# Gathering turned attention rows through a DRAM scratch: one write and four reads in place of sixteen transfers inside SBUF

## The chip, the core and the metric

The kernel runs on one core of a Trainium2 chip. The metric is device time in microseconds (us), the median of the runs. The compute engines are TensorE (PE in the profile, its weight loads PEld), VectorE (DVE), ScalarE (ACT) and GpSimd (POOL). Each works through its own instructions in order. SyncE (SP, its queue SPq) issues nearly all DMA transfers of this kernel, also in order: an issue that waits holds up every issue behind it. The transfers themselves run on sixteen DMA engines.

## The reference

One transformer block with adaptive layer norm, on 8 sequences of 1024 tokens and 512 channels, 16 heads of 32 channels, causal attention, all in float32:

```python
mod = jax.nn.silu(condition) @ Wada + bada
sh_a, sc_a, gt_a, sh_m, sc_m, gt_m = jnp.split(mod, 6, axis=1)
xn = _layernorm(x, g1, be1)
xm = xn * (1.0 + sc_a[:, None, :]) + sh_a[:, None, :]
x = x + gt_a[:, None, :] * _attention(xm, Wqkv, Wproj, bproj)
xn = _layernorm(x, g2, be2)
xm = xn * (1.0 + sc_m[:, None, :]) + sh_m[:, None, :]
h = jax.nn.gelu(xm @ W1 + b1, approximate=False)
x = x + gt_m[:, None, :] * (h @ W2 + b2)
```

## The kernel before

The 8192 rows are cut into 16 blocks of 512 tokens, two to a sequence. For each block the kernel normalizes the rows, brings them into a layout with channels on the partitions, modulates them (the tile xm_a), projects k, q and v, attends, projects out (Wproj), and does the same for the MLP half (xm_m, then up and down). Products with the large weights are done by Strassen's scheme: seven products of half-size blocks in place of eight, with sums of weight blocks (S1 to S4, kept in DRAM as kept_qkv, kept_up and kept_down) and differences of activation blocks (T1 to T4, the tile t_a).

The program is put in order by a planner inside the kernel. It keeps a clock for each engine (now), the planned time at which a value is there (written) and at which a buffer is free (left). Work that is to be interleaved is written as generators ("threads"): each yields what it needs next, and the planner advances the one whose wait is shortest. A number such as GATHERING = 16000 (ns) in written is an assumption on when a transfer will have landed. It moves instructions in the program's order; on the chip the engines wait on semaphores, whatever was assumed.

Weights come through a ring of nine buffers (RING, the tile w, 256 KB a piece). fetch() issues the next piece as soon as a buffer is released in the program's order, so on the chip a fetch (lines 338, 340 and 342) waits in SyncE's queue for the TensorE product that last read the buffer. In the same queue stand the x loads (line 389), the loads of the residual xr (line 1262), the gate rows (line 512) and the stores of finished rows to the output (line 1098). A store waits for the last addition to xr (line 161 on GpSimd: xr<-xr,p_d for the first pair of row tiles stored, xr<-xr,y_d for the second).

The attention rows of blocks 0 and 1 are turned by TensorE. Those of blocks 2 to 15 are "turned" without it, in fourteen turns, each in the generator turn():

1. The rows come in by four loads, so that partitions 32t to 32t+31 hold four rows each (line 389: the destination is 32 partitions by 4 by 512). They are normalized in place (the tile hat_a).
2. turn_tile (line 664): VectorE transposes blocks of 32 by 32, four instructions a block, from hat_a to xm_a, which serves as a scratch here.
3. The gathering (line 673): sixteen transfers, one for each pair of a group of 32 source partitions and a group of 32 target partitions, bring the pieces back to hat_a, 64 KB each.
4. modulated() then reads hat_a and writes xm_a, one chunk of channels at a time (line 726 on VectorE or line 732 on ScalarE), and forms the differences T1 to T4 (lines 740, 742, 158 and 161).

At about the time of a turn TensorE finishes the down products of an earlier block, then goes to the v products of the next and, between their last two, to the output projection (w with qT). Line 193 is the combine by VectorE that takes a product out of its PSUM bank.

The generators that matter are these:

Of the kernel before, what the change touches and what calls it, by code (L numbers as in the profile page):

```python
# [9 lines left out]
F32 = mybir.dt.float32  # L10
# [12 lines left out]
def kernel(  # L23
# [33 lines left out]
    nc = tc.nc  # L57
    B, T, D = x.shape
    HD = W1.shape[1]
    P = 128  # L60
# [3 lines left out]
    NTT = TB // P  # L64
# [18 lines left out]
    kept = ctx.enter_context(tc.tile_pool(name="kept", bufs=1, space=bass.MemoryType.DRAM))  # L83
# [10 lines left out]
    now = {"PE": 0.0, "DVE": 0.0, "ACT": 0.0, "POOL": 0.0}  # L94
    written, left = {}, {}
# [16 lines left out]
    def note(engine, ns, reads=(), writes=(), port=False):  # L112
        start = max(now[engine], due(reads, writes))
        if port:
            start = max([start] + [b for a, b in pool_spans if a <= start < b])
        end = start + ns
        now[engine] = end
        if engine == "POOL":
            pool_spans.append((start, end))
            del pool_spans[:-16]  # L120
        for k in reads:
            left[k] = max(left.get(k, 0.0), end + SYNC)
        for k in writes:
            written[k] = end + SYNC
        return end
# [102 lines left out]
    def mlp_steps(n):  # L228
        return [("u", n, i) for i in range(NQ)] + [("d", n, part) for part in range(4)]
# [9 lines left out]
    for w in range(1, NB):  # L239
        n = w - 1  # L240
        m = mlp_steps(n)
# [125 lines left out]
    rows = tmp.tile([P, TB], F32, tag="y", name="rows")[:n_rows, :P]  # L367
# [8 lines left out]
    Q = P // NTT  # L376
# [141 lines left out]
    def add_job(job, reads, first=False):  # L518

        at = sum(1 for other in jobs if other[2]) if first else len(jobs)  # L520
        jobs.insert(at, (job, reads, first))
# [134 lines left out]
    def turn(key, rows, xm):  # L656

        small_blocks = xm.rearrange("p c n -> p (c n)")
        by_tile = small_blocks.rearrange("p (m h t i) -> p h m t i", m=NTT, h=NC, t=NTT)
        written["blocks", key] = NEVER  # L660

        def turn_tile(t):
            into = by_tile[:, :, :, t, :]
            nc.vector.transpose(into, rows[:, t, :].rearrange("p (h m i) -> p h m i", m=NTT, i=Q))
            done = [("blocks", key)] if t == NTT - 1 else []
            note("DVE", 620, [("hat", key, t)], done)

        for t in range(NTT):
            add_job(lambda t=t: turn_tile(t), [("hat", key, t)], key[0] == "m")
        yield [("blocks", key)], []  # L670
        for m in range(NTT):
            for a in range(NTT):
                nc.sync.dma_start(rows[ts(m, Q), a, :], small_blocks[ts(a, Q), ts(m, D)])  # L673
        written["turned", key] = now["PE"] + GATHERING
        yield [("turned", key)], []

    GATHERING = 16000

    def modulated(key, gain, shift, b, guards):
        for t in ("B11", "B21", "B22", "T1", "T2", "T3", "T4"):  # L680
# [22 lines left out]
        if turned:  # L703
            yield from turn(key, got, xm)
# [1204 lines left out]
```

## Time and profile before

| | |
|---|---|
| median of 3 runs | 3577.96 us (3577.63 to 3582.41) |
| profiled execution, from its first to its last instruction | 3570.9 us |
| TensorE busy | 3495.3 us, 98% |
| VectorE / ScalarE / GpSimd busy | 61% / 33% / 58% |
| granted TensorE clock, mean | 0.997 |
| DMA queue of SyncE and ScalarE | 439.36 MB, 41.7% of sixteen engines' span |
| HBM read / written | 394.12 MB / 28.38 MB |

The profile is of one execution. Rows of the waits name who waited for whom, the total in us, how often, and the longest. Rows in order of time give start and duration in us, engine, line, operation, tiles (out<-in), shapes, count, and in brackets the idle time before and what ended it. Rows by stretch give the stretch and its length, then for each engine its busy time and instructions (PE, PEld, DVE, ACT, POOL), the granted clock, the share of time in which the DMA engines were busy, and GB/s. In the source view of a line three durations stand for the shortest, the median and the longest, in ns. Rows of the chain of waits give start, duration and what the end was waiting on. Issuing instructions on SyncE show the time of the issue, not of the transfer.

### The profile page before, as it was taken

To read this page: it belongs to the slowest core of one execution; us is meant where nothing else is said; L and a number is where in the kernel's file an instruction comes from. 1 tells how busy PE (TensorE), PEld (TensorE's weight loads), DVE (VectorE), ACT (ScalarE), POOL (GpSimd) and SP (SyncE) were. 2 spreads that over 40 slices of the span, in tenths; PEclk is the share of its full clock that TensorE was granted. 3 is DMA by queue.
4 is the path that set the end of the run, shared out by engine and by line. 5 is a ranking of instruction groups with operands and counts; after the bars stand their busy time and mean duration, and the time that the engine had idled before them with its cause. 6 is when DMAs were issued, how large, how long until landed. Compare 5 with 4: busy or idle time off the path is not lost.

```text
span 3570.9 us, 120927 instructions
## 1 busy us (share of the span) xinstructions
PE 3495.3 (98%) x54621; PEld 1749.3 (49%) x54621; DVE 2179.7 (61%) x2393; ACT 1187.1 (33%) x1232; POOL 2080.9 (58%) x2246
## 2 busy tenths in 40 slices
PE   8999899999999999999999999999999999999999
PEld 4444445445554445545454455544545445455445
DVE  5876575564755657465574656746666566565663
ACT  2334333242333513235142342423423134231421
POOL 2667746665466664667545775366762667526660
PEclk9999999999999999999999999999999999999999
DMA  6753433434434344433444334443344433434334
GB/s 200 235 174 93 128 93 110 135 105 138 115 109 131 108 141 113 135 107 105 142 118 146 99 101 141 120 140 102 102 131 124 140 105 104 126 111 140 91 113 137
DMA packets 318934, 447.12 MB, mean 125 GB/s; under 512 B 29516, under 2 KB 179852, under 8 KB 318164
## 3 DMA queue, kind: packets, MB, share of 16 engines
q1 hardware_dynamic: 318304, 439.36, 41.7%
q8 instruction: 430, 7.05, 0.8%
q14 instruction: 84, 0.69, 0.1%
q10 hardware_dynamic: 116, 0.03, 0.0%
HBM read 394.12 MB, written 28.38 MB: 118 GB/s over the span
## 4 chain that ended last, share of the span: by engine, by line
PE 88%; POOL 4%; DMA 3%; DVE 2%; SPq 2%; issue 1%; ACT 1%; ACTq 0%; DVEq 0%; POOLq 0%
PE bank L202 60%; PE sc L1511 8%; PE po L1644 7%; PE st L1604 7%; PE st L1592 2%; POOL pT L1734 2%; PE bank L1665 2%; DMA w<-in_L_cond_Wproj_dram 1%; PE bank L722 1%; SPq L673 1%; POOL hT L161 1%; DVE mx L1528 1%; DMA out_dram<-xr 0%; PE bank L1566 0%; DMA w<-in_L_cond_Wada_dram 0%
## 5 line engine op out<-in xcount | busy, mean ns | idle before, releaser
L1734 POOL TENSOR_TENSOR pT<-pT,pT 128x256 f32<-128x256 f32 (+3 forms) x1254 | 1215.4, 1005 | 335.5 <-PE po L1644 182.2
L1616 ACT ACTIVATE pT<-st 128x2048 f32<-128x2048 f32 x288 | 541.0, 1878 | 1171.6 <-PE st L1604 1074.2
L202 PE MATMUL bank<-w,hT 128*32 128x256 f32 x14336 | 813.0, 380 | 1.1 <-ACT rec L1674 0.9
L1528 DVE TENSOR_REDUCE mx<-sc 128x4 f32<-128x2048 f32 (+3 forms) x384 | 665.8, 1754 | 223.3 <-PE sc L1511 217.1
L202 PEld LDWEIGHTS bank<-w,hT 128*32 128x32 f32 x14336 | 453.0, 110 | 365.7 <-issue 81.0
L202 PE MATMUL bank<-xm_m,w 128*32 128x256 f32 x8192 | 498.2, 380 | 0.0
L202 PE MATMUL bank<-t_m,w 128*32 128x256 f32 x6144 | 383.4, 380 | 0.1
L1621 POOL TENSOR_SCALAR_AFFINE_SELECT pT<-pT 128x512 f32<-128x512 f32 x256 | 168.1, 675 | 344.6 <-ACT pT L1616 344.6
L202 PEld LDWEIGHTS bank<-xm_m,w 128*32 128x32 f32 x8192 | 257.2, 110 | 219.9 <-issue 54.6
L1511 PE MATMUL sc<-kT,qT 32*128 32x512 f32 (+3 forms) x3072 | 329.1, 520 | 2.7 <-DVE mx L1528 1.7
L1525 DVE TENSOR_TENSOR sc<-sc,mask 128x1024 f32<-128x1024 f32 (+1 forms) x160 | 162.7, 1017 | 265.5 <-PE sc L1511 177.5
L1644 PE MATMUL po<-pT,v 128*32 128x512 f32 (+3 forms) x3048 | 303.0, 492 | 2.1 <-POOL pT L1621 2.1
L1604 PE MATMUL st<-qT,kT 32*128 32x512 f32 (+3 forms) x3072 | 301.5, 488 | 0.0
L202 PEld LDWEIGHTS bank<-t_m,w 128*32 128x32 f32 x6144 | 190.2, 110 | 180.8 <-issue 58.1
L202 PE MATMUL bank<-w,qT 128*32 128x512 f32 x2048 | 240.7, 599 | 10.6 <-DMA w<-in_L_cond_Wproj_dram 10.5
L202 PE MATMUL bank<-xm_a,w 128*32 128x256 f32 x3968 | 246.0, 383 | 2.1 <-ACT p_k L188 2.0
L1683 DVE RECIPROCAL rec<-rec 128x128 f32<-128x128 f32 x256 | 224.5, 918 | 33.0 <-ACT rec L1674 33.0
L1511 PEld LDWEIGHTS sc<-kT,qT 32*128 32x128 f32 x3072 | 129.3, 183 | 173.1 <-ACT pT L1616 65.7
L202 PE MATMUL bank<-t_a,w 128*32 128x256 f32 x2944 | 189.6, 382 | 0.4 <-ACT xm_m L732 0.4
L193 DVE TENSOR_TENSOR hT<-bank,u_u 128x512 f32<-128x512 f32 x192 | 129.1, 684 | 98.2 <-PE bank L202 96.9
L1058 ACT ACTIVATE hT<-hT,cols 128x512 f32<-128x512 f32 x256 | 164.4, 711 | 54.6 <-DVE hT L193 54.0
L202 PEld LDWEIGHTS bank<-xm_a,w 128*32 128x32 f32 x3968 | 123.6, 110 | 110.8 <-issue 33.4
(216 smaller groups left out, 3405.6 us busy)
## 6 DMA issues: line engine op xcount, KB each, us to landing
w<-in_L_cond_W_dram SPq DMA_DIRECT2D x384, 256.0 KB
w<-kept_up_S SPq DMA_DIRECT2D x256, 256.0 KB
w<-kept_down_S SPq DMA_DIRECT2D x256, 256.0 KB
w<-kept_qkv_S SPq DMA_DIRECT2D x180, 256.0 KB
w<-in_L_cond_Wqkv_dram SPq DMA_DIRECT2D x147, 256.0 KB
hat_a<-in_x_dram SPq DMA_DIRECT2D x64, 256.0 KB
w<-in_L_cond_Wproj_dram SPq DMA_DIRECT2D x64, 256.0 KB
xr<-in_x_dram SPq DMA_DIRECT2D x64, 256.0 KB
```

The source lines that it names most:

```text
L193: nc.vector.tensor_tensor(out, src, other, op)
L202: nc.tensor.matmul(ps[r, :], columns, rhs, start=start, stop=stop, skip_group_check=True)
L1058: nc.scalar.activation(hT[:, i, :], hT[:, i, :], AF.Gelu, bias=cols[:, O_B1 + f : O_B1 + f + 1])
L1511: nc.tensor.matmul(sc[:, j, c0 : c0 + w], qTs[n][r, gg, ts(qt, P)], keys_of(n, kh)[r, gg, :w], start=True, stop=True, skip_group_check=True,)
L1525: nc.vector.tensor_tensor(place, place, shape_of.to_broadcast(place.shape), ALU.add)
L1528: nc.vector.tensor_reduce(maxima[n, gg][:, kh, qt, :], sc[:, :, c0 : c0 + w], axis=AX.X, op=ALU.max)
L1604: nc.tensor.matmul(st[:, j, c0 : c0 + w], kT[r, gg, ts(k % NTT, P)], qT[r, gg, TB - w :], start=False, stop=True, skip_group_check=True,)
L1616: nc.scalar.activation(pT[:, :, :used], st[:, :, :used], AF.Exp, scale=scale)
L1621: nc.gpsimd.affine_select(diagonal, diagonal, pattern=[[0, HPG], [1, P]], compare_op=ALU.is_ge, fill=0.0, base=0, channel_multiplier=-1,)
L1644: nc.tensor.matmul(po[r, TB - w :], v[:, k % NTT, g * P + j * hd : g * P + (j + 1) * hd], pT[:, j, c0 : c0 + w], start=(k == 0), stop=last ...
L1683: nc.vector.reciprocal(some, some)
L1734: nc.gpsimd.tensor_tensor(into, into, pT[:, j, c0 : c0 + w], ALU.add)
```

## The change

The sixteen transfers go. In their place the whole scratch (128 partitions by 8 KB) is written to a DRAM tile in one transfer, and four transfers read it back, each to 32 partitions, four rows of 2 KB to a partition, the form of the x loads. Two DRAM tiles alternate. Between write and reads the generator yields, so that the planner can put other work there; it assumes 8 us for the write and 8 us for the reads, where it assumed 16 us for the gathering. The reads wait on the chip for the write to have landed.

```diff
         yield [("blocks", key)], []
+        held = kept.tile([P, NTT * D], F32, tag=f"held_{turns[0] % 2}", name=f"held_{key}")
+        turns[0] += 1
+        nc.sync.dma_start(held, small_blocks)
+        written["held", key] = now["PE"] + HOLDING
+        yield [("held", key)], []
         for m in range(NTT):
-            for a in range(NTT):
-                nc.sync.dma_start(rows[ts(m, Q), a, :], small_blocks[ts(a, Q), ts(m, D)])
-        written["turned", key] = now["PE"] + GATHERING
+            some = held[:, ts(m, D)].rearrange("(a i) d -> i a d", i=Q)
+            nc.sync.dma_start(rows[ts(m, Q), :, :], some)
+        written["turned", key] = now["PE"] + HOLDING
         yield [("turned", key)], []
 
-    GATHERING = 16000
+    HOLDING = 8000
+    turns = [0]
```

In the order of instructions that results, the four reads stand four to nine transfers behind the write. For most blocks these are weight fetches and one or two pairs of output stores: in the turns of blocks 4 to 10 the reads come behind the first pair and ahead of the second, in those of blocks 11, 12 and 14 behind both, and in those of blocks 13 and 15 behind the last pair (the other being ahead of the write). On the compute engines the order is nearly the same as before; some dozen instructions at the modulation, the v combines and the output projection change places or engines, among them one chunk of the modulation in most blocks.

## The prediction

> **What bounds the kernel now.** I read the page first, then who waited for whom on TensorE, then the source view of the gather line, then SyncE in order of time around one turn.
>
> ```profile
> span 3570.9 us, 120927 instructions
> PE 3495.3 (98%) x54621; PEld 1749.3 (49%) x54621; DVE 2179.7 (61%) x2393; ACT 1187.1 (33%) x1232; POOL 2080.9 (58%) x2246
> ```
> ```profile
> PE bank L202 <- DMA w<-kept_qkv_S: 11.7, 7, 2.2
> PE bank L202 <- DMA w<-in_L_cond_Wproj_dram: 10.5, 12, 1.9
> ...
> PE bank L202 <- DMA w<-in_L_cond_Wqkv_dram: 3.7, 1, 3.7
> ```
>
> TensorE sets the end: it is idle for 75.6 us in all (3570.9 − 3495.3), so no edit that leaves its own work alone can win more. Three rows of its waits are for weight pieces, 11.7 + 10.5 + 3.7 = 25.9 us in 20 waits. Where they come from is seen on SyncE (start, duration, engine, line, operation, tiles, count) around the turn of block 7:
>
> ```profile
> L673 SPq DMA_DIRECT2D hat_a<-xm_a x224: 507/588/2077, 130.6 to 3051.9; - x112
> ```
> ```profile
> 1283.09 0.34 SPq L340 DMA_DIRECT2D w<-kept_qkv_S  x1
> 1283.57 11.66 SPq L673 DMA_DIRECT2D hat_a<-xm_a  x16
> 1295.32 1.02 SPq L340 DMA_DIRECT2D w<-kept_qkv_S  x2
> 1296.43 0.85 SPq L1098 DMA_DIRECT2D out_dram<-xr  x2
> ...
> 1297.89 0.89 SPq L338 DMA_DIRECT2D w<-in_L_cond_Wqkv_dram  x1
> 1298.87 1.05 SPq L342 DMA_DIRECT2D w<-in_L_cond_Wproj_dram  x2
> 1300.01 0.87 SPq L1098 DMA_DIRECT2D out_dram<-xr  x2
> 1300.97 1.79 SPq L342 DMA_DIRECT2D w<-in_L_cond_Wproj_dram  x2
> ```
> ```profile
> 1284.00:1295.00 11.00, 11.00 (x212) 6.62 (x208) 1.38 (x2) 0.00 (x0) 6.22 (x6) 1.00 0.47 116
> 1297.00:1302.00 5.00, 5.00 (x100) 2.84 (x93) 1.96 (x3) 3.37 (x5) 0.00 (x0) 1.00 0.99 314
> ```
>
> The sixteen issues hold SyncE for 11.66 us, while the DMA engines are busy 0.47 of the time at 116 GB/s (last two columns). Issue binds there, not data. The weight fetches, whose ring slots TensorE frees meanwhile, stand behind, go out in a burst that fills the engines (0.99), and TensorE runs dry some 20 us after the turn began:
>
> ```profile
> 1290.03 1.29 POOL L161 TENSOR_TENSOR xr<-xr,p_d 128x512 f32<-128x512 f32 x1
> 1295.64 1.28 POOL L161 TENSOR_TENSOR xr<-xr,y_d 128x512 f32<-128x512 f32 x1
> 1299.12 2.92 ACT L732 ACTIVATE xm_a<-hat_a,shifta,gaina 128x512 f32<-128x512 f32 x4
> 1303.41 1.28 DVE L193 TENSOR_TENSOR v<-bank,u_v 128x512 f32<-128x512 f32 x2
> 1305.22 1.92 PE L202 MATMUL bank<-w,qT 128*32 128x512 f32 x16 [1.37 <-DMA w<-in_L_cond_Wproj_dram]
> 1307.68 1.92 PE L202 MATMUL bank<-w,qT 128*32 128x512 f32 x16 [0.54 <-DMA w<-in_L_cond_Wproj_dram]
> 1309.42 1.91 PE L202 MATMUL bank<-w,t_a 128*32 128x256 f32 x32
> ```
>
> The same rows asked for by stretch, first 612 to 1960 us (the turns of blocks 4 to 10), then 2150 to 2835 us (blocks 11 to 14), then block 13's turn alone (2596 to 2630 us):
>
> ```profile
> PE bank L202 <- DMA w<-in_L_cond_Wproj_dram: 7.5, 9, 1.4
> PE bank L202 <- DMA w<-kept_qkv_S: 5.5, 3, 2.2
> ```
> ```profile
> PE bank L202 <- DMA w<-kept_qkv_S: 6.1, 4, 2.0
> PE bank L202 <- DMA w<-in_L_cond_Wproj_dram: 3.0, 3, 1.9
> ```
> ```profile
> PE bank L202 <- DMA w<-in_L_cond_Wproj_dram: 1.9, 1, 1.9
> ```
>
> So 13.0 us fall to blocks 4 to 10, 9.1 − 1.9 = 7.2 us to blocks 11, 12 and 14, 1.9 us to block 13, and the one wait for Wqkv, 3.7 us, to block 15; the turns of blocks 2 and 3 have none.
>
> **What the change removes.** 224 issues of 588 ns (median), 14 × 16. In their place stand 14 × 5. Their cost has near rows: the one transfer of 1 MB is the move of a whole kT, 0.51 us, and the four gathers have the form of the x loads (32 partitions by four rows of 2 KB), 1.84 us for four.
>
> ```profile
> 436.69 0.51 SPq L972 DMA_DIRECT2D kT<-kT_early  x1
> ```
> ```profile
> 1382.38 1.84 SPq L389 DMA_DIRECT2D hat_a<-in_x_dram  x4
> ```
> ```profile
> 438.00:440.00 2.00, 0.99 (x12) 0.31 (x8) 0.00 (x0) 1.00 (x1) 2.00 (x3) 1.00 1.00 376
> 1384.00:1388.00 4.00, 4.00 (x48) 1.25 (x40) 0.38 (x1) 2.84 (x3) 0.64 (x1) 1.00 1.02 237
> ```
>
> So 11.66 us of SyncE become 0.51 + 1.84 = 2.35 us. If nothing came in their place, all 25.9 us of waits for weights would go.
>
> **What it adds: data.** A turn moves 1.05 MB out and 1.05 MB back, where it moved 1.05 MB once. At the kT move's rate (376 GB/s, engines full) the write takes 2.8 us; at the x loads' rate (237 GB/s, also full, 32 partitions a transfer) the reads take 4.4 us, and I take 4.8 because fetches of the faster kind were mixed into that window. What a transfer costs beside its data: the last gather of block 15 was issued at 3051.88 and its reader began at 3054.52, 2.6 us with 0.3 us of data, so about 2.3 us.
>
> ```profile
> 3051.88 0.94 SPq L673 DMA_DIRECT2D hat_a<-xm_a  x1
> ```
> ```profile
> 3054.52 2.22 ACT L732 ACTIVATE xm_a<-hat_a,shifta,gaina 128x512 f32<-128x512 f32 x3 [6.76 <-DMA hat_a<-xm_a]
> ```
>
> **What it adds: two waits on SyncE.** First, the reads wait for the write. It lands 2.3 + 2.8 = 5.1 us after its issue on an empty queue. No row shows a 1 MB write to DRAM; the lower bound is this 5.1 us, the upper one the longest store in the chain (6.56 us for 256 KB in a full queue, its data replaced by the write's): 6.56 − 0.7 + 2.8 = 8.7 us. In the changed program four to nine transfers stand between write and reads, and among them, in most turns, a store to the output that waits for GpSimd. So SyncE comes to the reads 8 us or more behind the write, and I cost this wait at 0, its upper end at 0.7 us. Its cover is the work of those fetches and stores.
>
> ```profile
> 2820.36 6.56 DMA out_dram<-xr
> ```
>
> Second, those stores. They were reached after the sixteen issues, when their data were ready. Now SyncE reaches the first pair at once and must wait for xr<-xr,p_d, which in block 7's turn ends at 1291.32, 7.8 us after the write. The fetches behind this pair stay late, though by 7.8 and not 11.7 us. Worked for block 7: write 1283.57, stores 1291.3 to 1292.2, three fetches to 1293.6, reads 1293.6 to 1295.4. Ahead of them 5 × 0.26 MB need 3.5 us of engine time, a backlog of 1.3 us. The reads land at 1293.6 + 1.3 + 2.3 + 4.8 = 1302.0. The Wproj pieces, issued at 1293.1, 1295.4 and, behind the second stores (1296.9), about 1298.3 and 1298.8, land before 1305.9, against use at 1303.8 to 1306.4 without the gaps. That is enough, with under half a microsecond to spare for the last two.
>
> **What is late next.** The reads land at 1302.0, but ScalarE wanted them at 1299.12: it now stands 2.9 us. VectorE stands too, and queued behind its part of the modulation are the three differences and the combine v (1303.41), which frees what TensorE's next product (1309.42) writes to. From landing to the end of the first combine I count 2.2 (three ACTIVATEs) + 3 × 0.72 = 4.4 us, so 1306.4. TensorE without its two gaps comes to that product at 1309.42 − 1.91 = 1307.5: covered, by 1.1 us. Blocks 4 to 10 have the same order of work, and I take them as alike.
>
> In the turns of blocks 11, 12 and 14 the reads stand behind the second pair of stores too, which waits for xr<-xr,y_d. For block 11:
>
> ```profile
> 2156.50 10.95 SPq L673 DMA_DIRECT2D hat_a<-xm_a  x16
> ```
> ```profile
> 2166.83 1.29 POOL L161 TENSOR_TENSOR xr<-xr,y_d 128x512 f32<-128x512 f32 x1
> 2170.37 2.22 ACT L732 ACTIVATE xm_a<-hat_a,shifta,gaina 128x512 f32<-128x512 f32 x3
> 2173.36 1.93 PE L202 MATMUL bank<-w,t_a 128*32 128x256 f32 x32 [1.81 <-DMA w<-kept_qkv_S]
> 2180.55 1.91 PE L202 MATMUL bank<-w,t_a 128*32 128x256 f32 x32
> ```
>
> Data ready 2168.1, reads from 2169.0, landed at 2169.0 + 0.5 + 2.3 + 4.8 = 2176.6, combine done 2181.0; TensorE arrives at 2180.55 − 1.81 = 2178.7 and waits 2.3 us. Taken three times, 6.9 us of new stalls stand against the 7.2 us removed.
>
> **The sum.** Blocks 4 to 10: −13.0. Blocks 11, 12, 14: −7.2 + 6.9 = −0.3. Block 13: −1.9, block 15: −3.7 (both have their stores' data earlier). Together −18.9 us. Blocks 2 and 3 had no such wait to win and get later reads: between 0 and +3, taken +1.5. Left-over weight waits, since Wproj has under 0.5 us to spare in seven turns: between 0 and +4, taken +1.5. What TensorE then meets elsewhere because it comes earlier: 0 to +4, taken +0.9. Sum −15 us; by these bounds −8 to −19. Against the profiled span 3570.9 that is 3556; the runs' median, 3577.96, lies 7.06 us above that span, and I carry it over: 3563 us.
>
> **The rivals.**
> All of it goes: the stalls on the reads stay hidden, −25.9 us, 3552. For it: ScalarE is busy 33% of the span. Against: the 2.3 us worked out for block 11. Chance 0.2.
>
> Nothing is won, 3571 to 3585: the waits are those of the data burst, engines full at 0.99 from 1297 to 1302, and the extra 1.05 MB at 237 GB/s keeps it full; or the reads come 1 to 1.6 us later than I have them, which uses up the 1.1 us of cover in seven turns and costs its full length in the others. Against: the burst is the backlog of 11 us at 0.47. Chance 0.2. [...]
>
> Slower: the turned rows come late on ScalarE and VectorE. If the reads land 3 us later than worked out, blocks 4 to 10 lose 7 × (3 − 1.1) = 13 us, the seven other turns 7 × 3 = 21 us, 34 against the 15 won: +19, 3597; it decides from 1.6 us later on (7 × 0.5 + 7 × 1.6 = 15). The place would be the four reads behind the stores and the write. For it: their rate is little over half the write's. Against: the x loads of the same form show that rate. Chance 0.14.
>
> **How the numbers follow.** My forecast has 0.46, its own range is 3557 to 3570. Measurement tells 0.2% (7 us) from no change. Faster is the forecast and the full gain, 0.66; same 0.2; slower 0.14. The range 3551 to 3583 leaves out the slower case and a little at the lower end.
>
> **What would show it.** SyncE: five issues a turn, about 2.4 us together, and waits of the output stores on GpSimd of some 8 us each. TensorE's three weight rows under 5 us in all (25.9 now). A new wait of the modulation on ScalarE for hat_a<-held_a, about 3 us a turn and 6 in three of them. Wrong would be weight waits that stay above 15 us, a wait of SyncE for the write over 1 us a turn, or new TensorE waits on VectorE's v and t_a of over 15 us.

## The result, and the profile after

| | before | after |
|---|---|---|
| median of 6 runs each, us | 3576.38 (3570.8 to 3582.41) | 3563.38 (3559.5 to 3568.64) |
| ratio of after to before | | 0.9968 [0.9958, 0.9978] |
| profiled execution: time, span, us | span 3570.9 | 3568.64, span 3566.9 |

The change makes the kernel faster by 0.32%, 11.4 us (7.9 to 15.0). The forecast was 3563. How it came about is another matter, and the profile shows it.

First a caution on the two traces. The time of a run lies 1.74 us above its span (3568.64 − 3566.9), so the profiled execution of before was one of about 3572.6 us, 3.8 under its median, while that of after is the longest of its six, 5.3 above its median. The spans differ by only 4.0 us where the medians differ by 13.0. Rows of the two are compared here to see where waits went, not to add up to the gain.

The head of after's page (span; then busy time, share and count of each engine):

```profile
span 3566.9 us, 120690 instructions
PE 3490.9 (98%) x54621; PEld 1741.5 (49%) x54621; DVE 2181.1 (61%) x2395; ACT 1186.3 (33%) x1229; POOL 2081.8 (58%) x2247
```

TensorE is idle 76.0 us (3566.9 − 3490.9), where it was idle 75.6. TensorE's waits of after (us in total, times, longest):

```profile
PE bank L202 <- DMA w<-in_L_cond_Wproj_dram: 19.7, 14, 3.1
PE st L1598 <- DVE mx L1534: 10.1, 8, 3.0
...
PE bank L202 <- DVE v L193: 5.2, 3, 2.1
```

The rows for kept_qkv (11.7) and Wqkv (3.7) are gone. The one for Wproj has nearly doubled, from 10.5 to 19.7. A new one, for the combine v, takes 5.2. Together 24.9 us where there were 25.9: the pieces that were late first come in time, those that stand last in SyncE's queue are later than ever.

SyncE of after in order of time around the turn of block 7 (start, duration, line, tiles, count):

```profile
1272.23 0.34 SPq L673 DMA_DIRECT2D held_a<-xm_a  x1
1273.49 2.05 SPq L340 DMA_DIRECT2D w<-kept_qkv_S  x2
1280.02 0.82 SPq L1104 DMA_DIRECT2D out_dram<-xr  x2
1280.93 0.40 SPq L340 DMA_DIRECT2D w<-kept_qkv_S  x1
1281.42 0.40 SPq L338 DMA_DIRECT2D w<-in_L_cond_Wqkv_dram  x1
1281.92 0.47 SPq L342 DMA_DIRECT2D w<-in_L_cond_Wproj_dram  x1
1282.48 2.93 SPq L678 DMA_DIRECT2D hat_a<-held_a  x4
1285.50 0.38 SPq L342 DMA_DIRECT2D w<-in_L_cond_Wproj_dram  x1
1285.98 0.85 SPq L1104 DMA_DIRECT2D out_dram<-xr  x2
1286.92 1.59 SPq L342 DMA_DIRECT2D w<-in_L_cond_Wproj_dram  x2
```

The write goes out at 1272.23 in 0.34 us. Then SyncE waits for GpSimd until 1280.02, 7.8 us after the write, and the reads begin at 1282.48, 10.2 after it. Three of the four Wproj fetches stand behind the reads. What they meet there, in stretches of this turn (length; busy time and instructions of PE, PEld, DVE, ACT, POOL; clock, DMA share, GB/s):

```profile
1274.00:1276.00 2.00, 2.00 (x44) 1.19 (x40) 0.69 (x1) 0.00 (x0) 0.35 (x2) 1.00 1.08 453
1287.00:1291.00 4.00, 4.00 (x84) 2.40 (x76) 0.69 (x1) 0.59 (x1) 0.00 (x0) 1.00 1.04 221
```

In the first the write and two fetches pass at 453 GB/s; in the second, with the engines just as full, the reads to 32 partitions each pass at 221. ScalarE and TensorE at the end of the turn:

```profile
1291.67 2.22 ACT L738 ACTIVATE xm_a<-hat_a,shifta,gaina 128x512 f32<-128x512 f32 x3 [3.78 <-DMA hat_a<-held_a]
```
```profile
1295.39 1.92 PE L202 MATMUL bank<-w,qT 128*32 128x512 f32 x16 [1.25 <-DMA w<-in_L_cond_Wproj_dram]
```

The rows are used 19.4 us after the write (18.4 forecast), and TensorE still stands for a Wproj piece. Who waited, in after's waits of SyncE and of ScalarE:

```profile
SPq L1104 <- POOL xr L161: 80.5, 23, 9.0
SPq L1104 <- DVE xr L158: 24.8, 3, 11.2
```
```profile
ACT xm_a L738 <- DMA hat_a<-held_a: 72.8, 12, 10.6
```

SyncE stands 105 us on output stores (80.5 + 24.8), where it stood 47.5. No row has the reads waiting for the write to land.

One gain lies where none was sought, between 363 and 484 us, in block 3. First before, then after (length, PE busy and instructions, granted clock, DMA share, GB/s):

```profile
363.00:484.00 121.00, 110.44 (x1535) 0.94 0.35 110
```
```profile
363.00:484.00 121.00, 113.45 (x1655) 0.99 0.39 121
```

In the same 121 us after issues 120 more matmuls; at 121 / 1655 = 0.073 us each that is some 9 us (an estimate, for the matmuls differ in size). The clock is part of it: 0.05 of 121 us is 6 us. Before has waits of 2.68 and 3.20 us on mx and one of 2.00 on p_k here, and in the 4 us behind them the granted clock is 0.57, 0.50 and 0.58. In after the planner's order puts other work at these places.

How far after is ahead in its trace is seen from the start of each turn, its first transfer of line 673 (in us):

| turn of block | 3 | 4 | 7 | 9 | 10 | 11 | 12 | 15 |
|---|---|---|---|---|---|---|---|---|
| before | 363.52 | 618.93 | 1283.57 | 1720.48 | 1928.44 | 2156.50 | 2365.10 | 3041.29 |
| after | 363.29 | 611.63 | 1272.23 | 1706.27 | 1918.17 | 2149.78 | 2362.67 | 3039.27 |
| ahead | 0.23 | 7.30 | 11.34 | 14.21 | 10.27 | 6.72 | 2.43 | 2.02 |

Block 3 wins 7.1 us, blocks 4 to 8 win 6.9 more, and blocks 9 to 11 lose 11.8 again. In the turns of blocks 9 and 10 the reads go out 11.9 and 11.8 us behind the write and the rows are used 22.7 and 22.3 behind it; TensorE waits 3.4 and 3.9 us for Wproj there, against 1.2 in the turn of block 7. This execution of after was the longest of its six; whether the shorter ones lose as much here is not shown.

### The profile page after: what moved, and what is told of

The parts are those of the page before. It is cut to its first block, busy times and chain, and to the rows that moved or that the text cites. A ratio compares the mean times of both kernels' runs of the same rounds, so it can differ in the third digit from the quotient of the medians.

```text
span 3566.9 us, 120690 instructions
## 1 busy us (share of the span) xinstructions
PE 3490.9 (98%) x54621; PEld 1741.5 (49%) x54621; DVE 2181.1 (61%) x2395; ACT 1186.3 (33%) x1229; POOL 2081.8 (58%) x2247
## 4 chain that ended last, share of the span: by engine, by line
PE 88%; DMA 4%; POOL 3%; DVE 3%; ACT 1%; issue 1%; SPq 1%; ACTq 0%; DVEq 0%; POOLq 0%
PE bank L202 60%; PE sc L1517 8%; PE po L1650 7%; PE st L1610 7%; PE st L1598 3%; DMA w<-in_L_cond_Wproj_dram 2%; PE bank L1671 2%; POOL pT L1740 1%; DMA hat_a<-held_a 1%; PE bank L728 1%; DVE mx L1534 1%; POOL hT L161 1%; PE bank L1572 0%; DVE sc L1531 0%; DMA w<-in_L_cond_Wada_dram 0%
## 5 line engine op out<-in xcount | busy, mean ns | idle before, releaser
L202 PE MATMUL bank<-w,qT 128*32 128x512 f32 x2048 | 244.7, 606 | 21.2 <-DMA w<-in_L_cond_Wproj_dram 19.7
```

The source lines that it names most:

```text
L202: nc.tensor.matmul(ps[r, :], columns, rhs, start=start, stop=stop, skip_group_check=True)
```

## The experiments

All were timed in five rounds beside runs of the kernel before. A ratio is to the kernel before, with its 95% interval. A number of us behind it is the ratio times the median of before.

**1. Only the order that the planner makes.** The sixteen transfers stay in SBUF; the planned 16 us are cut into 8 and 8 with a yield between, as in the change.

```diff
-        written["turned", key] = now["PE"] + GATHERING
+        written["held", key] = now["PE"] + HOLDING
+        yield [("held", key)], []
+        written["turned", key] = now["PE"] + HOLDING
```

> The sixteen transfers stay; only the planner's two waits of 8 us take the place of the one of 16 us, so that the compute engines get nearly the changed program's order. Theory (SyncE's issues are what cost): the sixteen issues still hold SyncE 11 us a turn, TensorE's waits for weights stay near 26 us, time 3576 within 4 us. Rival (the gain comes from the other order of a few instructions, in block 3 above all): about 3565, with weight waits near 26 us.

Measured: 3570.09 against 3574.48, 0.9988 [0.9979, 0.9997], −4 us. TensorE's waits for weights are the old ones, and the stretch in block 3 has the new count:

```profile
PE bank L202 <- DMA w<-in_L_cond_Wproj_dram: 13.1, 16, 2.8
...
PE bank L202 <- DMA w<-kept_qkv_S: 5.6, 6, 1.4
...
PE bank L202 <- DMA w<-in_L_cond_Wqkv_dram: 3.8, 1, 3.8
```
```profile
363.00:484.00 121.00, 112.30 (x1650) 0.99 0.36 112
```

The time lies between the two expectations, with 22.5 us of weight waits still standing. From the turn of block 3 to that of block 4 this run takes 248.5 us, where before takes 255.4 and after 248.3. So about a third of the gain (4 of 11 us by the medians, with 1 to 7.5 in the interval) is the split of the planned time, which would have come without any DRAM.

**2. No gathering at all.** The write and the reads are left out, the plan stays; the modulation then works on rows that were not gathered.

> Leaves the gathering out: no write and no reads, the modulation reads the rows as the normalization left them. Order of the compute engines as in the changed kernel. Theory: the ceiling. SyncE still waits for GpSimd at the output stores, but the turned rows are there at once and no 2 MB a turn pass; TensorE's waits for weights fall from 19.7 us to under 6, those for VectorE's v to 0; 3545 to 3553. Rival (the waits for Wproj come from the stores' waits and the burst of Wproj, stores and residual loads, whatever the gathering does): weight waits stay above 12 us, 3557 to 3562.

Measured: 3522.44, 0.9857 [0.9844, 0.9871], −51 us, past both expectations.

```profile
span 3518.6 us, 120550 instructions
PE 3474.3 (99%) x54621; PEld 1742.9 (50%) x54621; DVE 2182.8 (62%) x2395; ACT 1184.5 (34%) x1229; POOL 2079.7 (59%) x2247
```

TensorE's idle time falls to 44.3 us, and its busy time by 21 against before with the same 54621 instructions. A wait is not all that a late piece costs; part of what more it costs is seen in the clock (last section). Leaving out the whole gathering is worth 51 us, twice the 25.9 that the waits for weights show; some 4 of the 51 are the order's, as in experiment 1.

**3. The reads right behind the write.** No yield between; the planner is told 16 us.

```diff
-        written["held", key] = now["PE"] + HOLDING
-        yield [("held", key)], []
...
-        written["turned", key] = now["PE"] + HOLDING
+        written["turned", key] = now["PE"] + 2 * HOLDING
```

> The four reads stand right behind the write on SyncE, ahead of the fetches and output stores; the planned time of use is the same 16 us. SyncE waits for the write to land (5 to 6 us by the prediction's sum), then for the stores. Theory (reads behind the stores come 3 to 8 us late and push ScalarE, VectorE and the Wproj fetches): reads land about 13 us after the write, before ScalarE wants them at 14 to 16; its waits for them fall from 72.8 us to under 15, TensorE's waits for weights from 19.7 to about 10, its waits for v to 0; 3553 to 3558. Rival (any wait of SyncE behind the write is paid by late weights): weight waits 20 us or more, 3563 or slower.

Measured: 3551.44, 0.9939 [0.9925, 0.9952], −22 us, and that without block 3's gain (1526 matmuls in its stretch). SyncE's waits, then ScalarE's:

```profile
SPq L676 <- DMA held_a<-xm_a: 64.7, 14, 6.1
```
```profile
ACT xm_a L736 <- DMA hat_a<-held_a: 8.3, 2, 6.6
```

Here SyncE does wait for the write, 4.6 us a turn, and it pays: ScalarE's wait for the rows drops from 72.8 to 8.3, and the weights cost 5.2 (Wproj 2.8, kept_qkv 2.4). The wait on the landed write is the cheaper one; the wait on GpSimd's sums, which the yield let in ahead of the reads, is the dear one.

**4. The slow side first.** The scratch in DRAM is held row by row. Four writes from 32 partitions each put the pieces in place, four reads bring 128 partitions each. The order on the queue is as in the change.

```diff
-        nc.sync.dma_start(held, small_blocks)
+        for a in range(NTT):
+            piece_a = small_blocks[ts(a, Q), :].rearrange("i (m d) -> i m d", d=D)
+            nc.sync.dma_start(held[a].rearrange("(m i) d -> i m d", i=Q), piece_a)
...
-        for m in range(NTT):
-            some = held[:, ts(m, D)].rearrange("(a i) d -> i a d", i=Q)
-            nc.sync.dma_start(rows[ts(m, Q), :, :], some)
+        for a in range(NTT):
+            nc.sync.dma_start(rows[:, a, :], held[a])
```

> The same data, but the write is cut into four of 32 partitions and each read goes to all 128 partitions: the slower form stands on the write's side, where 8 us are planned for it. Theory (the reads' low rate, 237 against 376 GB/s, makes them late and holds the fetches behind them): reads 2 us shorter, ScalarE's waits for them fall from 72.8 to about 50 us, weight waits from 19.7 to about 14, 3557 to 3560. Rival (a read's rate is hidden; only its place in the queue counts): within 2 us of the changed kernel's 3563.

Measured: 3541.15, 0.9906 [0.9893, 0.992], −34 us, better than either expectation. TensorE's waits and ScalarE's:

```profile
PE bank L202 <- DMA w<-in_L_cond_Wproj_dram: 3.8, 3, 2.0
...
PE bank L202 <- DVE v L193: 3.0, 3, 1.3
```
```profile
ACT xm_a L739 <- DMA hat_a<-held_a: 16.8, 7, 4.9
```

The stores stand ahead of the reads as in after, and still the Wproj row falls from 19.7 to 3.8. The bytes are the same: what changed is that the transfers on 32 partitions (issued from 1270.00 on in block 7; 277 and 244 GB/s from 1272 to 1276) now pass while SyncE waits for GpSimd (the stores go out at 1277.77) and little is behind them, and the rows are used 17.5 us behind the write in block 7 (19.4 in after).

**5. The sixteen transfers issued by ScalarE.** The kernel before, with `nc.scalar.dma_start` in place of `nc.sync.dma_start` on its gather line.

> The kernel before, but the sixteen transfers are issued on ScalarE's queue. Theory (the issues on SyncE make the weights late, and the fetches then wait for the stores' data alone): ScalarE is held some 10 us a turn where it has nothing to do but the modulation that needs these rows; TensorE's waits for weights fall from 25.9 to about 10 us or less; 3550 to 3562. Rival (the sixteen transfers delay the weights as data on the DMA engines, whoever issues them): weight waits stay above 20 us, 3572 or more.

Measured: 3569.97 against 3577.68, 0.9978 [0.9969, 0.9987], −8 us, where more was expected.

```profile
PE bank L202 <- ACT p_v L188: 25.2, 9, 8.1
...
PE bank L202 <- ACT rec L1674: 7.2, 2, 6.2
```
```profile
1275.95 13.98 ACTq L673 DMA_DIRECT2D hat_a<-xm_a  x16
1290.04 0.58 ACT L188 COPY p_v<-bank 128x512 f32<-128x512 f32 x1 [17.89 <-DMA w<-in_L_cond_Wqkv_dram]
```

No wait for weights is left in the turns, with the same sixteen transfers and the same bytes: the issues on SyncE were the cause. In the turns of blocks 4 and 5 TensorE waits for nothing that the profile lists, where before it stood 2.1 and 2.2 us for weights; in later turns it also stands for ScalarE's copies, which may hide a late piece, so for them the removal is less clean. For the issues take ScalarE 13.98 us now, and the copies that free TensorE's banks stand behind them.

**6. The stores off SyncE.** The change, with the output stores issued by GpSimd (`nc.gpsimd.dma_start` on line 1104).

> The changed kernel, but the output stores are issued by GpSimd, which makes their data, so that SyncE waits neither for GpSimd's xr nor queues the reads behind the stores. Theory (the reads are 3 to 8 us late because they stand behind stores that wait): reads at 8 to 9 us in every turn, ScalarE's waits for them from 72.8 to about 30 us, weight waits from 19.7 to about 8, no wait for v; 3547 to 3556, less what 64 issues cost GpSimd (about 1 us each, mostly hidden). Rival (the slow reads alone do it): ScalarE's waits stay above 55 us, 3560 or more.

Measured: 3551.81, 0.9931 [0.9917, 0.9945], −25 us. TensorE's waits:

```profile
PE bank L728 <- ACT hat_m L651: 6.2, 4, 2.3
PE po L1650 <- POOL pT L1627: 6.0, 4, 2.1
...
PE bank L202 <- DVE v_early L193: 5.2, 1, 5.2
PE bank L202 <- DMA w<-in_L_cond_Wproj_dram: 2.6, 4, 1.1
```

Wproj falls from 19.7 to 2.6 and ScalarE's wait from 72.8 to 41.1. GpSimd's issues give some back: the waits for pT and hat_m grew by 4.0 and 2.8, that for v_early by 4.3. GpSimd is busy 34.7 us longer than in after (2116.5 against 2081.8) with 62 more instructions (2309 against 2247), 0.56 us each; the 1 us an issue expected for it was an estimate that no run had shown.

**7. Slow side first, reads at once** (3 and 4 together).

> Four writes of 32 partitions with the four fast reads right behind them on SyncE. Theory: SyncE stands about 7 us for the last write (4.8 + 2.3), reads land at about 13 us as in the run with the reads at once, fetches behind are delayed by the fast reads less; between 3538 and 3550, near the slow-side-first run's 3541. Rival (a long stand of SyncE is what costs): slower than the 3551 of the reads at once.

Measured: 3536.11 against 3577.68, 0.9881 [0.9867, 0.9894], −43 us. SyncE waits for the writes 16.8 us in all, in 29 waits (64.7 in 14 in experiment 3): each read needs only its own quarter of the writes; no wait of ScalarE for the rows is left. The gain comes without that of block 3: that stretch has 1560 matmuls here, near before's 1535.

**8. Slow side first, stores off SyncE** (4 and 6 together).

> Both: slow side first, and output stores issued by GpSimd. Theory: reads in time in nearly every turn (ScalarE's waits for them under 10 us), weight waits under 3 us, 3528 to 3537, close to the 3522 without any gathering. Rival (GpSimd's issues hold its own chain, which SyncE's waits had hidden): 3541 or slower.

Measured: 3542.76, 0.9902 [0.9888, 0.9915], the same as 4 alone, as the rival had it. No wait for weights in the turns is left, but GpSimd's part comes back (v_early 5.2, hat_m 6.2). Experiments 4 and 6 remove much the same waits, and these can be removed only once.

**9. Slow side first, reads planned 4 us behind the write** and 12 more until the rows are due.

```diff
-        written["held", key] = now["PE"] + HOLDING
+        written["held", key] = now["PE"] + HOLDING // 2
...
-        written["turned", key] = now["PE"] + HOLDING
+        written["turned", key] = now["PE"] + 3 * HOLDING // 2
```

> The slow-side-first form with 4 us planned for the writes and 12 for the reads: the reads stand behind the first pair of stores in most turns, ahead of most fetches. Theory (the reads' place decides, and the new order of the compute engines is worth about 4 us by itself): SyncE waits less than 10 us in all for the writes, ScalarE less than 5 us for the rows, weight waits under 4 us; 3530 to 3536. Rival (the seven-microsecond stand costs nothing, and the order nothing either): 3536 to 3541.

Measured: 3534.33 against 3573.1, 0.9897 [0.988, 0.9913], −37 us, as theory had it. Its median is the lowest of the kernels that gather, but by the ratio to its own runs of before experiment 7 is ahead (0.9881); the intervals overlap, so the two are not told apart. The head of its page:

```profile
span 3530.9 us, 120758 instructions
PE 3481.8 (99%) x54621; PEld 1742.7 (49%) x54621; DVE 2181.7 (62%) x2395; ACT 1185.7 (34%) x1229; POOL 2081.9 (59%) x2247
```

Idle time of TensorE is 49.1 us, 4.8 above that of experiment 2, which gathers nothing. Kernels 7 and 9 both beat the change and the kernel before.

**10. The sixteen transfers in two runs of eight**, a yield and 6 us planned between, 10 us behind; all in SBUF.

> Sixteen transfers within SBUF as before, but in two runs of eight, 6 us planned between them, so that fetches and the first stores pass in between. No DRAM, no less issue time in all. Theory (the unbroken hold of SyncE makes the weights late): two holds of 5.5 us; weight waits from 25.9 to 10 to 15 us, but the second half is late for ScalarE; 3560 to 3568. Rival (the sum of the issue time counts): weight waits 22 us or more, 3570 or slower.

Measured: 3570.25 against 3573.1, 0.9996 [0.9985, 1.0007]: no change, as the rival had it.

```profile
PE bank L202 <- DMA w<-in_L_cond_Wproj_dram: 23.4, 20, 3.9
PE st L1594 <- DVE mx L1530: 16.7, 9, 6.7
```

As in the change, kept_qkv comes in time and Wproj pays (23.4, from 10.5); mx is waited for longer too (10.1 in after). Letting fetches in between moves the lateness down the queue; it does not remove it.

**11. The write doubled.** The change, and behind the write a second one of the same rows to another DRAM tile that nothing reads.

> The changed kernel with the write issued a second time, to DRAM that nobody reads: 1.05 MB more a turn, one issue more, no wait more. Theory (what costs is the reads' place and rate, in the 10 us after the stores; the time right behind the write is free): 2.8 us of the DMA engines in a stretch in which they are half idle; 3562 to 3567 against the changed kernel's 3563. Rival (bytes on the DMA engines cost wherever they pass): 14 turns of 1 to 2.8 us, 3575 to 3600.

Measured: 3584.31, 1.0028 [1.0019, 1.0038], 21 us above the change (0.0060 of 3576) or 1.5 us a turn. In block 7 the reads go out 10.2 us behind the write, as in after, but the rows are used at +21.7. First 4 us of after in which SyncE waits for the stores, then the 4 us that lie as far behind the write here, then the reads:

```profile
1275.50:1279.50 4.00, 4.00 (x80) 2.38 (x76) 0.41 (x1) 0.00 (x0) 3.35 (x3) 1.00 0.64 245
```
```profile
1285.00:1289.00 4.00, 4.00 (x80) 2.43 (x76) 0.47 (x1) 0.00 (x0) 3.30 (x3) 1.00 0.98 378
...
1292.00:1294.00 2.00, 2.00 (x44) 1.17 (x36) 0.43 (x1) 0.55 (x1) 1.42 (x2) 1.00 0.98 317
1294.00:1296.00 2.00, 2.00 (x44) 1.21 (x40) 0.69 (x1) 0.04 (x1) 1.14 (x1) 1.00 0.60 143
1296.00:1300.00 4.00, 4.00 (x80) 2.43 (x76) 0.69 (x1) 0.59 (x1) 0.00 (x0) 1.00 1.02 201
```

A megabyte that nothing waits for costs nearly twice what the change wins, as the rival had it. The time behind the write was not free: while SyncE waits for the stores the DMA engines are busy 0.64 of the time in after and 0.98 here, so they come to the fetches and the reads without the slack that after has. That is only part of an answer, for they also fall to 0.60 for 2 us between the issue of the reads and their use, and why is open.

**12. The reads in another order.** The change, with the target groups read 0, 2, 1, 3 in place of 0, 1, 2, 3.

```diff
-        for m in range(NTT):
+        for m in (0, 2, 1, 3):
```

> The changed kernel with one thing altered: the four reads go to the partition groups in the order 0, 2, 1, 3 in place of 0, 1, 2, 3; every instruction keeps its place on every engine. In the changed kernel the reads move 213 to 221 GB/s with the DMA engines fully busy, where the write moves 453. [...] Rival: the low rate is that of the 2 KB pieces or of reading DRAM, whatever the partitions, or the reads do not overlap enough: rate 200 to 225, rows at +19 to +20, Wproj 17 to 22, time 3560 to 3568, ratio 0.996 to 0.998.

Measured: 3552.56 against 3575.41, 0.9939 [0.9925, 0.9952], −22 us. Expected for a gain from the order were 3545 to 3557, waits for Wproj of 5 to 12 us and block 7's rows used at +18, the author's estimate, which no run had shown; the first two came, the third did not. TensorE's first row, and the 4 us that lie as far behind the write as after's 1287 to 1291:

```profile
PE bank L202 <- DMA w<-in_L_cond_Wproj_dram: 11.9, 11, 1.9
```
```profile
1282.50:1286.50 4.00, 4.00 (x80) 2.44 (x76) 0.69 (x1) 0.59 (x1) 0.00 (x0) 1.00 1.01 241
```

The rate is 241 GB/s where after's was 221, and in block 7 the rows are used at +19.4 as in after. In other turns they come sooner (block 9 at +19.8, where after has +22.7), ScalarE's waits for them fall from 72.8 to 62.9, and the Wproj pieces behind the reads gain most (11.9 from 19.7). So the order of the four reads matters. With the target partitions the order of addresses in DRAM changed too, so whether it is the partitions is not shown.

## Why the prediction was right or wrong

- **The cause, SyncE's issues: right.** Experiment 5 takes only them off SyncE, and every weight wait of the turns goes (in some turns beside new waits for ScalarE). After's issues are as costed: the write 0.34 us (0.51 forecast), the four reads 2.93 in block 7 (1.84), 3.3 us in this turn for the 11.66.
- **The write's landing, costed at nothing behind the stores: right.** No row of after has the reads waiting for it, and experiment 3, where they do, waits 4.6 us a turn (64.7 / 14) behind an issue of 0.34; 5.1 from the issue was worked out.
- **The wait on the stores: right in place and size.** 7.8 us in block 7, as forecast; 105 us over the span.
- **What is late next, in blocks 11, 12 and 14: right.** Three waits for v, 5.2 us together, against 3 × 2.3. In blocks 4 to 10 no wait for v came, as forecast, though ScalarE stood 3.8 us in block 7 (2.9 forecast). But these blocks were not alike, as the prediction took them: in blocks 9 and 10 ScalarE stood 7.0 and 6.6.
- **The left-over weight waits: the step that failed.** The sum gave them +1.5 us, at most 4; they are 19.7, and this was named as what would be wrong (above 15). Of these 7.3 fall to blocks 9 and 10, which the sum took to be like block 7. "That is enough, with under half a microsecond to spare" was the sentence. It let the Wproj fetches land at their usual delay, though three of four stand behind a second pair of stores or behind 1 MB of reads that pass at 221 GB/s. Experiments 6 and 3 let the reads and fetches go earlier (2.6 and 2.8 left), experiment 4 takes the slow data out of their way (3.8), 12 only mixes it better (11.9). Each alone brings most of it, so neither the stores nor the rate is the cause by itself: late and slow together are.
- **Blocks 2 and 3, costed at +1.5: wrong in sign.** Block 3 gains some 7 us in the trace by the other order, and experiment 1 shows 4 us over the whole kernel for the order alone. I had searched before's turns for waits on weights and rows, and a wait on mx or p_k was neither.
- **Wproj's 19.7 instead of 1.5 is 18 us too few won; block 3 makes up part.** The sum of −15 came out near −11 to −13 by errors of opposite sign, so that 3563 was met so closely is luck: the mechanism was right, and two terms of the sum were not. The 5.3 us by which the runs' median stood above before's profiled execution (beyond the 1.74 that every run adds) were carried over; with six runs of before it is 3.8.
- **The rivals.** "Nothing is won" was right that the data would bind: experiment 11 shows a price of 1.5 us for a megabyte. That before's waits were those of the data burst does not hold: experiment 5 passes the same sixteen transfers and takes only their issues, 11.66 us in block 7, off SyncE. The slower case needed the rows 1.6 us later than worked out in all turns; block 7 was 1.0 later, but blocks 9 and 10 were 4.2 and 3.9 later than worked out for block 7, and there the kernel fell back as that rival said. "All of it goes" and more is what the same data give when the slow side goes first: −34 to −43.
- **The ceiling.** The 75.6 us of idle time stand as a limit. But 25.9 us, the waits for weights, were too low as the full price of the gathering: experiment 2 gains 51.

## What to carry to other kernels

Here sixteen small transfers on a queue that also fetches weights, 11.66 us of issue in block 7's turn, made what stood behind them late (25.9 us of waits), and a wait let in between moved that lateness to the last fetch in line (Wproj, 10.5 to 19.7): follow the queue to its end before calling the rest "in time". Of a pair of transfers with a slow and a fast side, put the slow one where nothing stands behind it and nobody waits (here 22 us between two forms with the same bytes). When the change also moves the planner's due times, run the new order by itself: here it was about a third of the gain.

## What the runs showed of the hardware

**Behind 11 of 15 stalls of TensorE of 1.98 us or more the granted clock was 0.50 to 0.79.** The 15 are those between 60 and 3100 us of the two traces, before and after, and the clock is the mean of the 4 us behind each; behind the other four it was 1.00. None of the shorter stalls above 1 us has one below 1.00, but for two that lie next to a longer one. Block 3's stretch has three such stalls before (2.68, 2.00 and 3.20 us) and one after (2.65, with a clock of 0.68 behind it); the stretch's mean clock is 0.94 before and 0.99 after. In after one stands behind the waits in block 14 (start, duration, shapes, count, idle before; then length, PE busy and instructions, clock, DMA share, GB/s):

```profile
2823.43 2.69 PE L202 MATMUL bank<-w,qT 128*32 128x512 f32 x16 [2.15 <-DMA w<-in_L_cond_Wproj_dram]
2827.24 3.64 PE L202 MATMUL bank<-w,t_a 128*32 128x256 f32 x32 [1.12 <-DVE v L193]
```
```profile
2824.00:2826.00 2.00, 2.00 (x16) 0.62 1.05 369
2826.00:2828.00 2.00, 0.88 (x12) 0.50 1.05 387
2828.00:2832.00 4.00, 4.00 (x40) 0.59 0.60 200
```

Sixteen products take 2.69 us where they took 1.92 in block 7, and the clock is 0.50 to 0.62 for 8 us. Over the time in which TensorE is busy that loses about 0.38 × 2.00 + 0.50 × 0.88 + 0.41 × 4.00 = 2.8 us, behind 3.3 us of waits. This is an estimate from the three rows. So here late data cost nearly twice its wait, which the list of waits does not show, and this is part of why experiment 2 gains more than the waits: its mean clock is 0.999 where before's is 0.997, by estimate 0.002 × 3495.3 = 7 us. The clock had fallen, to 0.62 and then 0.50, behind the 2.15 us alone, before the 1.12 began.

**Reads to 32 partitions at a time passed at 221 GB/s, and their order mattered.** With the write it was 453. The two also differ in direction and in the size of their pieces, and no run here tells these apart. With the reads in the order 0, 2, 1, 3 (experiment 12) the rate in the same place was 241 GB/s, the waits for Wproj were 11.9 us in place of 19.7, and the time was 22 us below before's in place of 11.

**What stays open:** why the DMA engines fall to 0.60 between the issue and the use of the reads when the write is doubled (experiment 11), and how the rest of experiment 2's 51 us divides between waits, clock and longer products.
